# Layer 2's first product taken from layer 1's sums and rows, and stored blocks moved to the end of the pair loop

## The chip, the cores and the metric

The kernel runs on one core of one Trainium2 chip. The metric is the device time in microseconds of one execution, the median over several runs of the unchanged kernel: 566.83 us over 3 runs (566.69 to 569.11). Lower is better.

## The reference

The input is a matrix `x` of 3327 nodes by 64 features and a dense matrix `adj` (3327 x 3327, mostly zero). Four layers follow each other; each computes `x = layernorm(x + layer(x, adj))`. The change lies between the second and the third of them, which the reference numbers 1 and 2:

```python
# layer 1: hyperbolic attention
adj_att   = sigmoid(left + right.T) * adj
support_t = einsum('ij,ijd->id', adj_att, logmap(x_i, x_j))
x = layernorm(x + proj(expmap(x, support_t)))
# layer 2: two hops
for k in range(2):
    agg = adj @ x
    x = tanh(concatenate([agg, x], axis=1) @ W[k])
x = layernorm(x_in + x)
```

Since `concatenate([agg, x]) @ W[k]` is `adj @ (x @ W_top) + x @ W_bottom`, a hop of layer 2 needs the small product `x @ W_top` first, and then one pass over all of `adj`. "Layer 2's first product" is `x @ W_top` of hop 0.

## The kernel before, in words

The nodes are padded to 3328, which are 26 blocks of 128. A block of `adj` (transposed) is 128 rows of 3328 floats, 1.70 MB, one DMA from HBM. Four blocks (25 to 22, `kept`, `EARLY`) are loaded at the start and stay; all the others are fetched again in each layer. A row tile such as `x2`, `xc` or `lj` is [128, 26, 64]: one slot of 64 features for each block, blocks `b` and `b + 13` in neighbouring slots, so that a 128x128 transpose turns two blocks at once.

**Layer 1, the pair loop** (`near_sphere`, from L968). Two passes (`cp`) go over the 26 blocks; a pass takes half of the columns. One (pass, block) is a pair and has two tiles of 832 columns, 104 tiles in all. For each tile ACT makes the sigmoid (L1029, once a pair), POOL multiplies it by the block (`u`, L1040), PE makes distances (`pq`, L1053), DVE and ACT evaluate a cubic (`a` L1065, the square L1066, `v` L1074), and PE adds up `v` times the rows (`acc`, L1086). The order of blocks is written out in `order`; in both passes it begins with the four kept blocks. Streamed blocks go through four buffers (`at`, L1012) of a pool that stands beside the other work tiles. When the columns of a pass are summed, ACT copies them to `mT` (L1094), the sums, features by nodes. `ljT[0]` holds the nodes' rows in the same layout (differences to the last feature; the last feature's own row carries a norm term).

**Layer 1, the end** (`near_end`, L1286 to L1468). From `mT` PE makes the sums by node (`pm`, L1340) and their inner products with the rows (`pe`, L1350). ACT and DVE reduce them to about ten numbers per node. Then a chain of some 45 DVE instructions on [128, 26] tiles follows, with three ACT functions in it: a tanh (L1392) and two square roots (L1422). It ends in two factors per node, `al` and `be`: the layer's output is `x2 = al * M + be * xc` (L1463 to L1467), `M` the centred sums and `xc` the centred rows. Six matmuls of 512 columns whose result nobody reads (helper `awake`, L1326) stand in this chain. The same section centres layer 3's weights (`w3_dg`, L304).

**Layer 2** (`layers`, from L309). Hop 0 begins with `x2` turned by PE (`turned`, L345, copied by ACT, L349), the product with `W_top` (`top`, L355) copied to `lj` (L391), and the product with `W_bottom` added to the accumulators (`bottom`, L394). Then each block adds its 16 matmuls (`add`, L403). These beginnings are interleaved with the first two blocks. The blocks of hop 0 stand in `order`: four that were fetched ahead (`ready`, the `at_l` tiles), then a kept block and four streamed ones in turn (`bt_l` and `at_l`), 16 streamed in all, and two more kept ones at the end. Six blocks are asked for ahead of layer 2 by `blocks_ahead` (L1655): four `at_l` and two further `kept` ones (20, 21, pool `late`).

**What sets the order.** Each engine's instructions stand in the order written in the source within `manual_schedule`. DMAs of blocks all go through SP's queue, in order: one that waits for its buffer holds all behind it. Pools that are opened over the space of closed ones make the new tile's first writer wait for the last readers of the old one.

Of the kernel before, what the change touches and what calls it, by code (L numbers as in the profile page):

```python
# [15 lines left out]
ALU = mybir.AluOpType  # L16
# [57 lines left out]
def kernel(  # L74
# [234 lines left out]
    def layers(ctx, x2, x3, kept, ready, ahead_ctx, strm):  # L309
# [67 lines left out]
        with tc.tile_pool(name="l2p", bufs=2, space=PSUM, reuse_waits="tile") as l2p:  # L377
            for k in range(2):
# [49 lines left out]
                if k == 0:  # L428
# [20 lines left out]
                else:  # L449
# [13 lines left out]
                for i, jb in enumerate(order):  # L463
# [6 lines left out]
                    for c in range(CPH):  # L470
                        add(c, jb)
                    if k and jb in held and len(held) == 2:
                        for q in range(AHEAD + 3):
                            masks(q)
# [384 lines left out]
    with tc.tile_pool(name="l1", bufs=1) as l1:  # L859

        def l1_stat(name):
            return l1.tile([P, NB], F32, name=name)

        aa, g1, ga, xn, rxn, gs, gs2, gk, lpn = (
            l1_stat(name) for name in ("aa", "g1", "ga", "xn", "rxn", "gs", "gs2", "gk", "lpn")
# [107 lines left out]
        def near_sphere(mT, xm, sq_e, t_e):  # L973
# [3 lines left out]
            with tc.tile_pool(name="n1", bufs=1, reuse_waits="tile") as n1, tc.tile_pool(  # L977
# [3 lines left out]
            ) as n1c, ExitStack() as pairs:  # L981
                first_ps = ExitStack()
# [5 lines left out]
                ljT = [n1.tile([P, HALF], F32, name=f"ljT_{k}") for k in range(2)]  # L988
# [18 lines left out]
                def load(cp, jb):  # L1007
                    of = slice(cp * 2 * CW, (cp + 1) * 2 * CW)
                    if jb in kept:
                        return kept[jb].rearrange("p (h k) -> p h k", h=2)[:, :, of]  # L1010
                    at = n1w.tile([P, 2, 2 * CW], F32, tag="at", bufs=4, name=f"at1_{cp}_{jb}")
                    rows = adjT[jb * P : (jb + 1) * P, :].rearrange("p (h k) -> p h k", h=2)  # L1012
                    nc.sync.dma_start(at, rows[:, :, of])
                    return at

                tiles = [(cp, jb, ci) for cp in range(2) for jb in order for ci in range(2)]
# [53 lines left out]
                def gather(t, extra=()):  # L1070
# [10 lines left out]
                    if jb == order[0]:  # L1081
# [3 lines left out]
                    for h in range(2):  # L1085
                        nc.tensor.matmul(  # L1086
                            accs[cp, ci][h * D : (h + 1) * D, :], xv[:, slot(jb), :], w[:, h, :],
                            start=(jb == order[0]), stop=(jb == order[-1]),
# [3 lines left out]
                    if jb == order[-1]:  # L1092
# [102 lines left out]
                with tc.manual_schedule(  # L1195
# [47 lines left out]
                    for t in range(len(tiles)):  # L1243
# [13 lines left out]
                        if t == len(tiles) - 4:  # L1257
                            of = slice(0, 2 * CW)
                            nc.gpsimd.tensor_tensor(xm[:, of], mT[:, of], ljT[0][:, of], ALU.mult)
                        if t == len(tiles) - 3:  # L1260
# [15 lines left out]
                    of = slice(2 * CW, 3 * CW)  # L1276
                    nc.gpsimd.tensor_tensor(xm[:, of], mT[:, of], ljT[0][:, of], ALU.mult)
                    layer_3_constants()

                    nc.vector.tensor_scalar(gs, g1, MIN_NORM, -256.0, ALU.max, ALU.mult)  # L1280
                    vec(gk, gs, ga, ALU.mult)
                    vec(gs2, gs, gs, ALU.mult)
# [3 lines left out]
        def near_end(mT, xm, sq_e, t_e, x2):  # L1286
# [3 lines left out]
            with tc.tile_pool(name="l1e", bufs=1) as l1e, tc.tile_pool(  # L1290
                name="l1t", bufs=1, space=PSUM
            ) as l1t, tc.tile_pool(name="l1m", bufs=5, space=PSUM) as l1m:

                prod = l1e.tile([P, NB, D], F32, name="prod_xm")
                sqm = l1e.tile([P, NB, D], F32, name="prod_mm")
# [14 lines left out]
                def both(a, scalar, b, tag, op0, op1):  # L1310
# [5 lines left out]
                    engines={mybir.EngineType.PE, mybir.EngineType.Activation, mybir.EngineType.DVE}  # L1316
                )
                in_order.__enter__()
                gss = of(mul, gs, s, "gss")
                gks = both(gk, -2.0, s, "gks", mul, mul)  # L1320
                aav = lin(aa, 1.0 / D, LN_EPS, "aav")
                idle = l1t.tile([P, 512], F32, name="idle_e")

                def awake(t):

                    nc.tensor.matmul(  # L1326
                        idle[:NB, :], t, xc[:, :8].rearrange("p n d -> p (n d)"),
                        start=True, stop=True,
                    )

                gt = st("gt")
                p, q = st("p"), st("q")
                nc.vector.tensor_reduce(q[:, :12], sq_e, axis=AX.X, op=add)
                pms = {}

                def both_products(g, n):
# [9 lines left out]
                for g, n in threes[2:]:  # L1346
                    both_products(g, n)
                pe = l1t.tile([P, 9, 2], F32, name="pe")
                for k in range(9):
                    nc.tensor.matmul(  # L1350
                        pe[:, k], xm[:, k * P : (k + 1) * P], but_last, start=True, stop=True
                    )
                for g, n in threes[:2]:
                    both_products(g, n)
                for g, n in threes[2:]:
                    m = pms[g][:, :, :P].rearrange("p n (h d) -> p n h d", h=2)
                    nc.scalar.activation(by_half(sqm)[:, g : g + n], m, AF.Square)
                    if g > 6:
                        vec(by_half(prod)[:, g : g + n], m, by_half(xc)[:, g : g + n], mul)
                vec(gt[:, :12], t_e, gk[:, :12], mul)  # L1360
                for g, n in threes[2:]:
                    sl = slice(2 * g, 2 * (g + n))
# [4 lines left out]
                nc.vector.tensor_reduce(p[:, 18:], prod[:, 18:], axis=AX.X, op=add)  # L1367
                nc.vector.tensor_reduce(q[:, 12:], sqm[:, 12:], axis=AX.X, op=add)
                nc.vector.tensor_copy(p[:, :18], pe.rearrange("p n h -> p (n h)"))

                k = of(mul, p, gks, "k")
                vec(k, k, gt, add)
                gp = of(mul, p, gss, "gp")
                vec(p, p, s, mul)
# [7 lines left out]
                awake(u2)  # L1382
                centred_weights(l1t)
# [6 lines left out]
                awake(th)  # L1390
# [3 lines left out]
                nc.scalar.activation(warm_e[:, :1], ones, AF.Sqrt)  # L1394
                uy = of(mul, th, ux, "uy")
# [7 lines left out]
                al = of(mul, ca, gs, "al")  # L1403
                vec(be, be, ck, sub)
                alp = of(mul, al, p, "alp")
                bea = of(mul, be, aa, "bea")
                al2 = of(mul, al, al, "al2")
                n2 = both(alp, 2.0, bea, "n2", mul, add)
                vec(al2, al2, q, mul)
                vec(n2, n2, be, mul)  # L1410
                vec(alp, alp, bea, add)
                vec(n2, n2, al2, add)
                awake(n2)
                root = lin(n2, MIN_NORM * MIN_NORM, None, "root", ALU.max, ALU.bypass)
                dn = lin(y2, 1.0, None, "dn", add, ALU.bypass)
                stt(dn, uy, 2.0, dn, op0=mul, op1=add)
                sca(dn, dn, MIN_NORM, None, ALU.max)

                def rsqrt2(v, tag):

                    r0 = st(f"{tag}_r")
                    nc.scalar.activation(r0, v, AF.Sqrt)  # L1422
                    awake(v)
                    nc.vector.reciprocal(r0, r0)
                    t = of(mul, v, r0, f"{tag}_t")
                    vec(t, t, r0, mul)
                    stt(t, t, -3.0, r0, op0=add, op1=mul)
                    return t


                r0 = st("rdn")
                nc.vector.reciprocal(r0, dn)
                on = rsqrt2(root, "on")
# [296 lines left out]
```

## Time and profile before

| | us |
|---|---|
| median of 3 runs | 566.83 (566.69 to 569.11) |
| profiled execution, its own time | 566.58 |
| its span, first to last instruction | 564.9 |
| PE busy | 527.5 (93%) |
| DVE busy | 362.7 (64%) |
| ACT busy | 277.3 (49%) |
| POOL busy | 216.7 (38%) |
| HBM read | 143.23 MB, 255 GB/s over the span |

A page of the profile gives busy times by engine, the same in 40 slices of the span (14.1 us each), the chain of work that ended last, and groups of instructions by line. The timeline lists instructions with start and duration; `[2.66 <-DVE e_n]` behind a row is the idle time of that engine before it and who ended it. Several equal instructions in a row are merged (`x16`). `PEclk` is the clock that TensorE was granted, 1.00 being full. A name with a number stripped, such as `at_l` or `w_dg`, is the source's `at_l2` or `w2_dg`.

### The profile page before, as it was taken

The page shows a single profiled execution, that of the slowest core. Times are in us where ns is not written, and L with a number is a line of the kernel's source. Part 1 is how long each engine was busy: PE and PEld are TensorE (multiplying, and loading weights), DVE is VectorE, ACT ScalarE, POOL GpSimd, SP SyncE. Part 2 cuts the span into 40 slices and gives each one's busy share as a digit, 9 for nine tenths or more (in the row PEclk, how much of TensorE's full clock was granted, in tenths as well). Part 3 has the DMA queues.
Part 4 walks back from the last instruction along what each step waited for, and adds up shares of the span by engine and source line. Part 5 has one row for each costly group of instructions (what it writes and reads, how often), then busy time and mean ns, then how long its engine had stood idle before and what let it go on. Part 6 is the DMA issues. An engine that isn't in the chain of part 4 may idle for free.

```text
span 564.9 us, 7457 instructions
## 1 busy us (share of the span) xinstructions
PE 527.5 (93%) x2827; PEld 221.9 (39%) x2827; DVE 362.7 (64%) x527; ACT 277.3 (49%) x330; POOL 216.7 (38%) x134
## 2 busy tenths in 40 slices
PE   8899989999999999779999999999999999999992
PEld 5523222222222223444444454443455555545542
DVE  6899999999999999750000010400378888787834
ACT  4899999999999997350000000000274333343311
POOL 3799999999999999110000000000011000000000
PEclk9899999999999999999999999999999999999997
DMA  8986766660576671999999219999609986689801
GB/s 293 356 282 202 237 201 219 208 231 0 188 236 203 222 238 35 386 430 424 427 426 424 113 49 411 425 426 382 243 0 307 359 303 244 214 267 338 302 2 36
DMA packets 34037, 145.27 MB, mean 257 GB/s; under 512 B 10285, under 2 KB 11975, under 8 KB 28871
## 3 DMA queue, kind: packets, MB, share of 16 engines
q1 hardware_dynamic: 31655, 144.11, 69.5%
q10 hardware_dynamic: 2336, 0.59, 0.5%
q8 instruction: 24, 0.39, 0.3%
q14 instruction: 22, 0.18, 0.1%
HBM read 143.23 MB, written 0.87 MB: 255 GB/s over the span
## 4 chain that ended last, share of the span: by engine, by line
PE 63%; DVE 20%; ACT 8%; issue 5%; DMA 2%; DVEq 0%; POOL 0%; POOLq 0%
PE cnt L403 23%; PE pq L1053 12%; DVE v L1074 12%; PE cnt L498 11%; PE acc L694 6%; ACT sg L1029 4%; PE acc L709 3%; ACT pq L1066 2%; DVE a L1065 2%; DMA at_l<-in_adjT 2%; PE pn_l L355 1%; DVE w L511 1%; PE cnt L394 1%; DVE mask L337 1%; PE idle L889 1%
## 5 line engine op out<-in xcount | busy, mean ns | idle before, releaser
L1040 POOL TENSOR_TENSOR u<-sg,at 128x832 f32<-128x832 f32 x88 | 169.8, 1960 | 3.2 <-ACT sg L1029 2.7
L1053 PE MATMUL pq<-riT,ljT 64*128 64x416 f32 x416 | 100.2, 560 | 15.2 <-DVE v L1074 6.3
L1065 DVE SCALAR_TENSOR_TENSOR a<-pq,dl,u 128x832 f32<-128x832 f32 x104 | 111.8, 1076 | 3.0 <-PE pq L1053 2.9
L1066 ACT ACTIVATE pq<-pq,al,gas 128x832 f32<-128x832 f32 x104 | 104.9, 1010 | 15.2 <-DVE a L1065 14.2
L1074 DVE SCALAR_TENSOR_TENSOR v<-pq,a 128x832 f32<-128x832 f32 x104 | 105.5, 1014 | 1.1 <-ACT pq L1066 0.7
L1086 PE MATMUL acc<-v,xv 128*64 128x416 f32 x416 | 95.4, 538 | 0.1
L1029 ACT ACTIVATE sg<-lb,rb 128x1664 f32<-128x1664 f32 (+1 forms) x53 | 87.3, 1647 | 0.1
L403 PE MATMUL cnt<-at_l,lj 128*64 128x416 f32 x480 | 86.3, 513 | 0.6 <-DMA at_l<-in_adjT 0.6
L513 ACT ACTIVATE w<-cnt 128x832 int16<-128x832 f32 x55 | 47.2, 863 | 71.5 <-PE cnt L498 71.4
L478 ACT ACTIVATE hT<-cnt 128x416 f32<-128x416 f32 x8 | 4.1, 517 | 148.6 <-PE cnt L403 148.6
L625 POOL TENSOR_TENSOR s<-sq,s 128x384 bf16<-128x384 f32 (+1 forms) x4 | 4.1, 1026 | 188.0 <-ACT s L624 188.0
L511 DVE TENSOR_SCALAR w<-cnt 128x832 int16<-128x832 f32 x49 | 50.1, 1023 | 25.8 <-PE cnt L498 24.5
L1053 PEld LDWEIGHTS pq<-riT,ljT 64*128 64x128 f32 x416 | 31.5, 184 | 88.3 <-DVE v L1074 83.0
L391 DVE COPY lj<-pn_l 128x384 f32<-128x384 f32 (+2 forms) x8 | 4.3, 541 | 85.2 <-PE pn_l L355 85.2
L403 PEld LDWEIGHTS cnt<-at_l,lj 128*64 128x64 f32 x480 | 34.0, 137 | 50.0 <-issue 47.7
L498 PE MATMUL cnt<-mask,tri 128*128 128x416 bf16 x208 | 53.5, 339 | 0.1
L694 PE MATMUL acc<-w,s 128*128 128x416 bf16 x208 | 52.6, 339 | 0.5 <-DVE hid L766 0.5
L498 PE MATMUL cnt<-mask,rest 128*128 128x416 bf16 x200 | 51.6, 340 | 1.2 <-ACT w L513 0.6
L1086 PEld LDWEIGHTS acc<-v,xv 128*64 128x64 f32 x416 | 20.6, 134 | 61.0 <-issue 57.7
L337 DVE TENSOR_SCALAR mask<-ah 128x1664 bf16<-128x1664 f32 x42 | 43.4, 1033 | 0.0
L403 PE MATMUL cnt<-kept,lj 128*64 128x416 f32 x192 | 35.5, 513 | 0.0
L1040 POOL TENSOR_TENSOR u<-sg,kept 128x832 f32<-128x832 f32 x16 | 30.9, 1962 | 3.8 <-ACT sg L1029 3.8
(283 smaller groups left out, 390.2 us busy)
## 6 DMA issues: line engine op xcount, KB each, us to landing
at_l<-in_adjT SPq DMA_DIRECT2D x26, 1664.0 KB, 12.0
at<-in_adjT SPq DMA_DIRECT2D x44, 832.0 KB, 4.9
ah<-in_adjT SPq DMA_DIRECT2D x42, 832.0 KB, 6.4
bt_l<-in_adjT SPq DMA_DIRECT2D x8, 1664.0 KB, 10.0
kept<-in_adjT SPq DMA_DIRECT2D x6, 1664.0 KB, 8.8
lb<-lf_rows SPq DMA_DIRECT2D x2, 384.0 KB, 4.4
ljT<-ljT SPq DMA_DIRECT2D x4, 128.0 KB, 6.4
x<-in_x ACTq DMA_DIRECT2D x1, 416.0 KB, 5.4
```

The costliest lines, as they stand in the source:

```text
L337: nc.vector.tensor_scalar(mask[q], at, 0.0, None, ALU.not_equal)
L403: nc.tensor.matmul(acc[c][h * D : (h + 1) * D, :], hw[:, slot(jb), :], blocks[jb][:, o : o + CW], start=c not in begun, stop=last, skip_gr ...
L498: nc.tensor.matmul(cnt[c][:, e, :], mat, mask[q][:, of], start=start, stop=(mat is tri), skip_group_check=True,)
L511: nc.vector.tensor_scalar(w.bitcast(I16), cnt[c], 0.0, None, ALU.max)
L694: nc.tensor.matmul(acc[h, c][:, e, :], s12[:, slot(jb)].rearrange("p t d -> p (t d)"), ws[q, c][:, e, :], start=first, stop=last,)
L1029: nc.scalar.activation(sg[:, :, of], lbs[:, :, of], AF.Sigmoid, bias=rb[:, sl : sl + 1])
L1040: nc.gpsimd.tensor_tensor(u, sg[:, :, of], at[:, :, of], ALU.mult)
L1053: nc.tensor.matmul(pq[:, h, :], ljT[h != jb // NBH][rows, of], riT[rows, ch * CW : (ch + 1) * CW], start=True, stop=True,)
L1065: stt(a_s[t], pqs[t], dl[:, one], us.pop(t), op0=ALU.add, op1=ALU.mult)
L1066: nc.scalar.activation(pqs[t], pqs[t], AF.Square, bias=al[:, one], scale=gas[:, one])
L1074: stt(w, pqs.pop(t), CUBIC_REST, a_s.pop(t), op0=ALU.add, op1=ALU.mult)
L1086: nc.tensor.matmul(accs[cp, ci][h * D : (h + 1) * D, :], xv[:, slot(jb), :], w[:, h, :], start=(jb == order[0]), stop=(jb == order[-1]),)
```

## The change

1. Hop 0's `x2 @ W_top` is no longer made from the finished `x2`. PE multiplies the rows `ljT` by the centred `W_top` (`x_w`) and the sums `mT` by the centred and turned `W_top` (`m_w`) inside `near_end`, where the chain of small instructions runs; the two factors per node (now `alpha`, `beta`) are then put on both by DVE, straight into `lj`. `x2` itself is computed behind that, and its transposes and `bottom` come after the fourth, fifth and sixth block of hop 0.
2. `near_end` is put into one written order for POOL too: the products with `xm` are made by DVE, `pe` covers all 13 column blocks (26 matmuls for 18), the six matmuls of `awake` are gone, the chain between tanh and the second root is written otherwise, constants of the chain are made by POOL at the end of the pair loop, and ACT takes copies of `M` and of the products between its functions.
3. In the second pass the four kept blocks come last. The streamed `at` buffers move to a pool of their own (`n1r`, right side), and the two `late` blocks (20, 21) are asked for first and take that space.

The diff, cut to its core:

```diff
+                n1r = pairs.enter_context(
+                    tc.tile_pool(name="n1r", bufs=4, side="right", reuse_waits="tile")
+                )
-                    at = n1w.tile([P, 2, 2 * CW], F32, tag="at", bufs=4, name=f"at1_{cp}_{jb}")
+                    at = n1r.tile([P, 2, 2 * CW], F32, tag="at", name=f"at1_{cp}_{jb}")
-                tiles = [(cp, jb, ci) for cp in range(2) for jb in order for ci in range(2)]
+                orders = (order, sorted(order, key=lambda jb: jb in kept))
+                tiles = [(cp, jb, ci) for cp in range(2) for jb in orders[cp] for ci in range(2)]
...
+                            gp.tensor_scalar(gs, g1, MIN_NORM, -256.0, ALU.max, ALU.mult)
+                            gp.tensor_tensor(gk, gs, ga, ALU.mult)
...
+                            gp.tensor_tensor(rows_63, but_last[:, :1], but_last[:, 1:], ALU.add)
-                    of = slice(2 * CW, 3 * CW)
-                    nc.gpsimd.tensor_tensor(xm[:, of], mT[:, of], ljT[0][:, of], ALU.mult)
-                    layer_3_constants()
...
+                nc.vector.tensor_reduce(q[:, :12], sq_e, axis=AX.X, op=add)
+                x_times_m(2)
+                x_times_m(3)
+                m_and_t(6, 3)
+                m_and_t(9, 3)
+                m_and_t(12, 1)
+                p_of(0, NBH)
...
+                m_out(6, 3)
+                m_out(9, 3)
+                m_out(12, 1)
+                nc.scalar.activation(w3_dg, w3_dg, AF.Copy, scale=float(2**27))
...
+                first = in_bank("first_w")
+                nc.tensor.transpose(first[:, :P], all_m[:, :P], ident)
+                nc.tensor.matmul(
+                    first[:, P : 2 * P], center, w2_dg[:, 0, :], start=True, stop=True
+                )
+                m_and_t(0, 3)
...
+                nc.scalar.copy(all_mT, first[:, :P])
+                nc.scalar.activation(w_x, first[:, P : 2 * P], AF.Copy, scale=rows_63)
+                second = in_bank("second_w")
+                nc.tensor.matmul(second[:, :P], all_mT, w2_dg[:, 0, :], start=True, stop=True)
+                nc.tensor.matmul(second[:, P : 2 * P], center, w3_dg, start=True, stop=True)
+                xs = [in_bank(f"x_w_{g}") for g, _ in fours[:2]]
+                times(xs[0], ljT, w_x, *fours[0])
+                times(xs[1], ljT, w_x, *fours[1])
+                m_and_t(3, 3)
+                last_x = in_bank("x_w_12")
+                times(last_x, ljT, w_x, *fours[3])
...
-                awake(u2)
-                centred_weights(l1t)
...
                 nc.scalar.activation(th, arg, AF.Tanh, scale=-1.0)
                 warm_e = st("warm")
                 nc.scalar.activation(warm_e[:, :1], ones, AF.Sqrt)
+                nc.scalar.copy(w_m, second[:, :P])
+                m_out(0, 3)
...
+                r0, r = table_root(root, "on")
+                x_out(xs[0], *fours[0])
+                x_out(xs[1], *fours[1])
...
+                r0, t = table_root(var, "ln")
+                m_out(3, 3)
+                nc.scalar.copy(w3_dg, second[:, P : 2 * P])
+                x_out(last_x, *fours[3])
+                rest_x = in_bank("x_w_8")
+                mw = {b: in_bank(f"m_w_{b}") for b in (0, 3, 1, 2)}
+                times(mw[0], mT, w_m, *fours[0])
+                times(rest_x, ljT, w_x, *fours[2])
+                x_out(rest_x, *fours[2])
+                for b in (3, 1, 2):
+                    times(mw[b], mT, w_m, *fours[b])
...
+                for b, g, n in ((0, 0, 1), (0, 1, 3), (3, 12, 1), (1, 4, 4), (2, 8, 4)):
+                    sl = slots(g, n)
+                    pt = mw[b].rearrange("p (n d) -> p n d", d=D)
+                    pt = pt[:, sl.start - 8 * b : sl.stop - 8 * b]
+                    vec(pt, pt, one(alpha, sl), mul)
+                    vec(lj[:, sl], lj[:, sl], one(beta, sl), mul)
+                    vec(lj[:, sl], lj[:, sl], pt, add)
+                for g, n in threes:
+                    sl = slots(g, n)
+                    vec(x2[:, sl], x2[:, sl], one(alpha, sl), mul)
+                    vec(xc[:, sl], xc[:, sl], one(beta, sl), mul)
+                    vec(x2[:, sl], x2[:, sl], xc[:, sl], add)
...
+            for jb in range(NB - EARLY - LATE, NB - EARLY):
+                all_kept[jb] = block(late, jb, name=f"kept_{jb}")
             for jb in range(UNDER_WAY):
                 ready[jb] = block(strm, jb, tag="at", name=f"at_l2_0_{jb}")
...
-                if k == 0:
+                if k == 0 and not begun_here:
...
+                    if k == 0 and begun_here:
+                        if i == 3:
+                            turned(0)
+                            turned(1)
+                        if i == 4:
+                            turned(2)
+                            turned(3)
+                            turned(4)
+                        if i == 5:
+                            for c in range(CPH):
+                                bottom(c)
```

Here `times(pt, rows, w, g, n)` makes `n` products of 128x128, `x_out` and `m_out` are ACT copies out of PSUM, and `in_bank` takes one of four banks of the pool `l1w` in turn, so that a fifth tile waits until the first has been copied out. `m_and_t`, `p_of` and `t_of` are the former `both_products`, the `pe` loop and the `gt` products under new names.

## The prediction

> **What bounds the kernel now.** I read the page's slices first, then the table by stage, then the timeline from the end of the pair loop to the first blocks of layer 2.
>
> ```profile
> PE   8899989999999999779999999999999999999992
> 225.00:248.00 23.00, 16.51 (x93) 9.32 (x93) 18.30 (x87) 10.44 (x32) 3.90 (x7) 1.00 0.96 395
> 270.00:326.00 56.00, 56.00 (x324) 23.04 (x322) 0.00 (x0) 1.55 (x3) 0.00 (x0) 1.00 0.80 337
> 336.00:384.00 48.00, 48.00 (x276) 19.65 (x276) 6.08 (x7) 0.00 (x0) 0.00 (x0) 1.00 0.99 410
> ```
>
> The columns of a stage are its length, then busy time and count of PE, weight loads, DVE, ACT and POOL, the granted clock, the DMA share and GB/s. In layer 2 PE is never idle (56 of 56, 48 of 48). The dip is slices 17 and 18 (two 7s): between pair loop and layer 2 PE has 16.5 busy of 23, and much of that is matmuls nobody reads. There the chain of waits runs through small DVE instructions:
>
> ```profile
> 232.52 0.19 DVE L1302 TENSOR_TENSOR e_k<-e_p,e_gks 128x26 f32<-128x26 f32 x1
> 235.60 0.27 ACT L305 COPY both_m<-pw 128x128 f32<-128x128 f32 x1 [5.89 <-issue]
> 235.76 0.23 ACT L1392 ACTIVATE e_tanh<-e_th 128x26 f32<-128x26 f32 x1
> 238.31 0.23 ACT L1422 ACTIVATE e_on_r<-e_root 128x26 f32<-128x26 f32 x1 [0.81 <-DVE e_root L1307]
> 241.19 0.23 ACT L1422 ACTIVATE e_ln_r<-e_n 128x26 f32<-128x26 f32 x1 [2.66 <-DVE e_n L1441]
> 242.56 0.18 DVE L1445 SCALAR_TENSOR_TENSOR e_al<-e_ln_t,e_al 128x26 f32<-128x26 f32 x1
> 248.41 3.01 PE L403 MATMUL cnt<-at_l,lj 128*64 128x416 f32 x16
> 251.35 0.55 PE L345 MATMUL pt_x<-ident,x 128*128 128x128 f32 x3
> 256.66 2.96 PE L394 MATMUL cnt<-xc,w_dg 128*128 128x416 f32 x8
> ```
>
> Seen here: the factors per node are there at 242.7, and it takes 5.85 us more (multiply, turn, copy, product, copy) until the first block of layer 2 starts. Whatever starts that block earlier moves all that follows, because PE is full from there.
>
> **The change, part by part.**
>
> *Start of the chain.* `pe` grows to 26 matmuls. L1350's 18 took 2.07 us, so 0.107 each and 0.25 for the last; from 229.07 that ends at 232.0. DVE has finished its reductions by 231.1 (it drops the 832-element `prod` and 0.67 of a reduction, takes 2 x 0.59 for two products of 416), so the chain begins at 232.1 for 232.52. In before the tanh argument was ready at 234.78 but the tanh ran at 235.76: ACT held the copy L305, which waited for a PE product behind an `awake`. Now ACT has 1.2 us of `M` copies (0.48, 0.48, 0.27, released by `pe` from 231.2 on), then 0.2 to 0.27 each for `w3_dg`, `all_mT`, `w_x`, and is free at 233.5. The argument, 2.2 us after the chain's start, is the later one: tanh at 234.35, **1.4 us earlier**.
>
> *Tanh to first root.* 22 small instructions for 18, at the 0.11 to 0.22 that the rows show: 3.0 us for 2.55, **0.45 later**. Behind the tanh ACT loads a table (1.28), then copies `w_m` and one `M` part (0.75): free at 236.8, root wanted at 237.35.
>
> *First to second root.* One reciprocal (0.32) and 6 dependent steps instead of two reciprocals and 12: 1.7 us for 2.88, **1.2 earlier**. In it ACT does two copies of 512 (0.58 each, as L1164 shows), ending at 238.75; the second root is wanted at 239.05. That cover is 0.3 us thin; without it the rest would be the root's delay. To `alpha` 1.27 instead of 1.37: it starts at **240.3**, for 242.56.
>
> *Factors to first block.* The first 128 columns of `lj` need three DVE instructions (0.29 is the row of a 128x128 multiply out of PSUM, and 0.2 between starts): ready at 241.25. But PE comes later. Its last 17 products (`m_w` 13, `x_w` 4) stand ahead of the first block in its queue and begin when the first bank is copied out, at 238.2. L1340's 7 products took 1.86, 0.25 each: 4.25, and some 0.3 for two waits on ACT copies: **PE is free at 242.8**. This, and not the chain, starts the first block: 248.41 - 242.8 = **5.6 us earlier**. The bounds: if the products overlap their waits fully, DVE's 241.25 (7.2 us); if each product costs what L355's 3 did with their fill and drain (0.94, 0.31 each), 243.8 (4.6 us). I take 242.8, since the products run in groups of four, nearer to the seven of L1340.
>
> *Inside hop 0.* Removed: 13 `top` products and their waits, 2.04 us at 251.35 and 0.33 at 256.33. Added there: 13 transposes at 0.17 (L345, 3 in 0.52), 2.2 us. `bottom` (2.9) stays. DVE's five triples of `lj` and five of `x2` end near 253, before the fourth block ends (254). I count **0.3 earlier**; if the transposes wait for each other's ACT copies (two banks, 0.48 a copy), 0.5 later.
>
> *Stored blocks last.* A pair costs the same either way (POOL's multiply is 1960 ns with `at`, 1962 with `kept`). The last streamed pair now ends four pairs (15.4 us) earlier, so blocks 20 and 21 are asked for at about 207.8 instead of 223.26 and 229.36, while DMA was idle. No time by itself; it pays for the earlier start:
>
> ```profile
> 222.00:224.00 2.00, 1.90 (x12) 0.40 (x8) 2.00 (x3) 1.02 (x1) 2.00 (x2) 1.00 0.00 0
> 227.55 1.77 SPq L209 DMA_DIRECT2D at_l<-in_adjT  x4
> 312.00:316.00 4.00, 4.00 (x26) 1.70 (x24) 0.00 (x0) 0.00 (x0) 0.00 (x0) 1.00 0.60 253
> ```
>
> The four `at_l` still wait for the last tile's products, so they are asked for at 227.55 as now; SP holds nothing else. Data flow from 228.8. A block of 1.70 MB at 425 GB/s takes 4.0 us (4.1 for the first four): `at_l` 0 is there at 233, the sixteenth streamed block of hop 0, the twentieth in this queue, at 228.8 + 16.4 + 64 = 309.2. PE wants it after 23 blocks of 2.8 (384 matmuls took 67.2 us, 16 each), transposes and `bottom`: 242.8 + 64.4 + 5.1 = 312.3. Before, the last ended near 314.4 and was wanted at 318.4. So 3.1 us of margin are left of 4; with the two early blocks still in this queue (8 us) there would be none. In hop 1 the buffers come free by PE's own progress; it moves as a whole.
>
> At this place the Trainium skill speaks against the change. Measured here are 424 to 432 GB/s in the stages from 240 on. "DMA: Bandwidth & Descriptors", section "Where 436 GB/s comes from", gives about 358 GB/s as the limit of HBM reads per core; at that rate, by estimate, 20 blocks would take some 95 us, the last would land at 324, and hop 0 would end later than before. The measured rate decides.
>
> *POOL.* Eight small instructions (0.22 to 0.28 each by L1209 to L1211) behind the `xm` product that ends at 225.15: done at 227.3, first read at 229.4. The two casts for layer 3 stand ahead of the pair loop in the built order, 0.6 us in 3.6 + 2.1 us of POOL idleness. Nothing.
>
> *TensorE's clock.* The six `awake` matmuls (1.04 us each) go, and `pe` moves only 2 columns a matmul.
>
> ```profile
> 12.00:14.00 2.00, 1.77 (x14) 1.35 (x14) 1.70 (x9) 1.48 (x2) 0.00 (x0) 0.98 1.01 433
> 14.00:16.00 2.00, 2.00 (x10) 2.00 (x11) 1.41 (x13) 0.71 (x2) 0.73 (x3) 0.50 1.13 296
> ```
>
> After 24 matmuls of 4 columns (10.8 to 13) the granted clock fell to 0.50, and it stayed there from 13.9 to 17.2. `pe` is such a stretch, of 2.9 us, so a stretch at half clock from about 232 is likelier than not; it slows `x_w`, which have 1.2 us of slack at 237, by up to 1.7 us. I charge **0.4**. "TensorE: Matmul & The Clock Gate", Part 1, tells the same story by windows of about 3.4 us that run free; by that rule the products (full from 232 to 237 and from 238.2 on) would bring the clock back after one window, and the loss on `x_w` would be at most 1.7.
>
> **Sum.** 5.6 + 0.3 - 0.4 = 5.5 us off the profiled execution's 566.58 (span 564.9 and 1.7 around it): **561.1 us**. The median of the runs shown is 566.83, 0.25 above; I leave the forecast at 561.1.
>
> **Rivals.**
> 1. *The transfers end last in hop 0.* For: only 3.1 us of margin, and 223 to 240 ran at 343 GB/s. Against: that stretch had one block in flight at first, and now four queue at once. At 400 GB/s a block costs 4.26, the last lands at 314.0, 1.7 past PE's wish: 562.8.
> 2. *Half clock over the last 17 products.* For: the queue of PE is empty from about 237 to 238.2 and the `awake`s are gone. Against: 5 us of products before. Price 1.7 to 2.5: 563.2.
> 3. *Half clock from 232 into layer 2*, the slower side. If products of 128 columns count too little, 19 products from 232.1 at 0.5 us end at 241.6, the last 17 at 250.3, and the first block loses 1.7 more: 252 against 248.4, 3.5 slower: 570. It decides when the clock is not back to 1.00 by about 238. Against: between 234 and 242 PE was busy 5.1 us of 8 in before and kept 1.00.
> 4. *The early blocks do nothing*, since their request sits behind a later wait: the order of SP's queue puts only `at` blocks before them, so this costs nothing by the order; were it so, the last block would land 8 us later, 4.9 past PE's wish: 566.0, no change. Counted with rival 1.
>
> **How the numbers follow.** Forecast (560 to 562.4) 0.70; rival 1, 0.11; rival 2, 0.11; rival 3, 0.08. The range reaches from DVE's bound (7.2 us off, 559.4) to rival 2 with its dearer price (564.2). Faster by over 0.5% (about what a measurement of this kernel can tell from no change) is below 564.0: the forecast, nearly all of rival 1 and half of rival 2, 0.86; within 0.5%: 0.06; slower: 0.08.
>
> **What would show it.** `e_tanh` near 234.4, the roots near 237.4 and 239.1, `alpha` near 240.3; the first `cnt` matmul of layer 2 near 242.8, right behind the last `m_w`; `kept` asked for at 208; no DMA wait of PE in hop 0; hop 0 of 78 us. Wrong would be: ACT's copies ending behind a root's argument, a clock of 0.5 beyond 236, or `cnt` waiting for `at_l` or `bt_l`.

## The result, and the profile after

The changed kernel takes **561.99 us** (median of 4 runs, 561.51 to 562.48) beside 567.28 for the kernel before on the same chip (566.69 to 569.11): ratio 0.990, 95% interval 0.988 to 0.993. The forecast was 561.1, the range 559.4 to 564.2. In a second set of runs (4) the same kernel gave 561.47 (560.66 to 562.12), ratio 0.988 (0.985 to 0.991). The profiled execution took 562.28 with a span of 560.5, so the span lost 4.4 us, not the 5.5 of the prediction.

First the page of the kernel after, then three stages (length, busy time of PE, weight loads, DVE, ACT, POOL, clock, DMA share, GB/s):

```profile
PE   8989989999999999999999999998989999999992
PEclk9899999999999999899999999999999999999997
225.00:248.00 23.00, 23.00 (x164) 17.94 (x164) 19.50 (x83) 10.20 (x27) 2.13 (x9) 0.93 0.85 346
270.00:326.00 56.00, 55.84 (x320) 23.81 (x318) 1.38 (x2) 2.07 (x4) 0.00 (x0) 1.00 0.72 302
336.00:384.00 48.00, 48.00 (x278) 19.65 (x276) 5.79 (x6) 0.00 (x0) 0.00 (x0) 1.00 1.01 424
```

The two 7s in PE's row are gone: PE is busy for all 23 us of the seam, the stretch between the pair loop and layer 2. Two 8s are new behind it, in slices 28 and 30; the first of these is the end of hop 1. The seam in the timeline:

```profile
232.19 0.19 DVE L1440 TENSOR_TENSOR e_k<-pe,gks 128x26 f32<-128x26 f32 x1 [1.19 <-PE pe L1391]
234.31 0.23 ACT L1479 ACTIVATE e_tanh<-e_th 128x26 f32<-128x26 f32 x1 [1.12 <-DVE e_th L1477]
237.12 0.23 ACT L1512 ACTIVATE e_on_s<-e_root 128x26 f32<-128x26 f32 x1 [0.54 <-DVE e_root L1338]
237.25 1.05 ACT L1417 COPY lj<-x_w 128x512 f32<-128x512 f32 x2
237.87 1.16 PE L1411 MATMUL m_w<-w_m,mT 128*128 128x128 f32 x8
238.74 0.23 ACT L1512 ACTIVATE e_ln_s<-e_var 128x26 f32<-128x26 f32 x1 [0.44 <-DVE e_var L1525]
239.75 2.17 PE L1411 MATMUL m_w<-w_m,mT 128*128 128x128 f32 x18
240.01 0.19 DVE L1543 SCALAR_TENSOR_TENSOR dl<-e_n_r,e_al 128x26 f32<-128x26 f32 x1
240.83 0.29 DVE L1552 TENSOR_TENSOR lj<-lj,m_w 128x128 f32<-128x128 f32 x1
241.86 11.39 PE L403 MATMUL cnt<-at_l,lj 128*64 128x416 f32 x64
```

DVE's first rows are ready at 240.83 + 0.29 = 241.1, and the first block starts at **241.86**, behind the last `m_w` (before: 248.41). What follows, in the order of time: the requests of the two stored blocks and of the first four streamed ones, and the only two waits of PE for a transfer in layer 2; below them the one such wait of the kernel before.

```profile
207.86 0.84 SPq L209 DMA_DIRECT2D kept<-in_adjT  x2
227.62 2.15 SPq L209 DMA_DIRECT2D at_l<-in_adjT  x4
312.10 3.01 PE L403 MATMUL cnt<-at_l,lj 128*64 128x416 f32 x16 [0.16 <-DMA at_l<-in_adjT]
391.15 3.01 PE L403 MATMUL cnt<-at_l,lj 128*64 128x416 f32 x16 [2.15 <-DMA at_l<-in_adjT]
```

```profile
395.72 3.01 PE L403 MATMUL cnt<-at_l,lj 128*64 128x416 f32 x16 [0.59 <-DMA at_l<-in_adjT]
```

So the account of the span is: the first block starts 6.55 earlier; hop 0 (first block to hop 1's first product, L355) takes 78.77 for 78.33, 0.44 lost, so that hop 1 starts at 320.6 for 326.7; the wait in hop 1 is 2.15 for 0.59, **1.56 lost**; layer 3 and the rest take 169.3 for 169.1, 0.17 lost. 6.55 - 0.44 - 1.56 - 0.17 = 4.4.

### The profile page after: what moved, and what is told of

The parts are those of the page before. It is cut to its first block, busy times and chain, and to the rows that moved or that the text cites. A ratio compares the mean times of both kernels' runs of the same rounds, so it can differ in the third digit from the quotient of the medians.

```text
span 560.5 us, 7513 instructions
## 1 busy us (share of the span) xinstructions
PE 527.3 (94%) x2854; PEld 226.6 (40%) x2854; DVE 368.2 (66%) x532; ACT 278.1 (50%) x328; POOL 215.7 (38%) x138
## 4 chain that ended last, share of the span: by engine, by line
PE 61%; DVE 20%; ACT 8%; DMA 6%; issue 3%; DVEq 0%
PE cnt L403 20%; PE pq L1075 12%; DVE v L1096 12%; PE cnt L513 11%; PE acc L709 6%; DMA at_l<-in_adjT 5%; ACT sg L1051 4%; PE acc L724 3%; ACT pq L1088 3%; DVE a L1087 2%; DVE w L526 1%; PE cnt L394 1%; DVE mask L337 1%; DMA x<-in_x 1%; PE pm L1367 1%
## 5 line engine op out<-in xcount | busy, mean ns | idle before, releaser
L391 DVE COPY lj<-pn_l 128x512 f32<-128x512 f32 (+1 forms) x4 | 2.4, 592 | 73.9 <-PE pn_l L355 73.9
L1108 PEld LDWEIGHTS acc<-v,xv 128*64 128x64 f32 x416 | 20.6, 134 | 61.0 <-issue 57.8
```

The source lines that it names most:

```text
L1108: nc.tensor.matmul(accs[cp, ci][h * D : (h + 1) * D, :], xv[:, slot(jb), :], w[:, h, :], start=(jb == orders[cp][0]), stop=(jb == orders[c ...
```

## The experiments

Theory after the profile: (a) the product from layer 1's sums brings the first block forward, and PE's own work sets it there; (b) the early blocks pay only because the first block comes early; (c) the loss in hop 1 is the tail of the stream, which the loading of instructions delays. Rivals: the product alone is the gain; the half clock costs part of it; the loss in hop 1 is another block's or belongs to the execution. "Chain start" is `e_k`.

**1. Stored blocks not last** (early blocks undone, all else as after).

```diff
-orders = (order, sorted(order, key=lambda jb: jb in kept))
+orders = (order, order)
```

> The changed kernel with one thing undone: the second pass begins with the four kept blocks again, as in the first. Theory (the early request of blocks 20 and 21 pays for the earlier start): both are asked for at about 223.3 instead of 207.9, so 22 blocks of some 4.05 us stand in one stream from 224.5; the last streamed block of hop 0 lands at 314 plus the lag of the slowest DMA engine (about 3 us), and PE wants it at 312: a wait of 3 to 5 us in hop 0, 565 to 567 us. Rival (transfers are hidden anyway): no wait, 562.0.

565.15 us (564.16 to 566.15), ratio to before 0.9945 (0.992 to 0.997). The first block is as early as after (242.34), `kept` is asked for at 223.80, and PE waits in hop 0 four times where the kernel after waits 0.16. The rows of PE:

```profile
252.13 3.01 PE L403 MATMUL cnt<-at_l,lj 128*64 128x416 f32 x16 [0.98 <-DMA at_l<-in_adjT]
300.12 3.02 PE L403 MATMUL cnt<-at_l,lj 128*64 128x416 f32 x16 [0.24 <-DMA at_l<-in_adjT]
312.11 3.01 PE L403 MATMUL cnt<-at_l,lj 128*64 128x416 f32 x16 [0.60 <-DMA at_l<-in_adjT]
316.09 3.01 PE L403 MATMUL cnt<-at_l,lj 128*64 128x416 f32 x16 [0.96 <-DMA at_l<-in_adjT]
```

The sum of these waits is 2.8 us; hop 0 as a whole takes 82.3 us for 78.8, and the difference of the medians is 3.2. The two early blocks are worth that, where the first block comes early.

**2. First product from `x2`** (`x_w`, `m_w` and what serves them removed, `x2` made first, turned and multiplied as in the kernel before; the early blocks stay).

```diff
-times(xs[0], ljT, w_x, *fours[0])
...
-x_out(xs[0], *fours[0])
...
-for b in (3, 1, 2):
-    times(mw[b], mT, w_m, *fours[b])
...
-layers(x2, xc, True, *blocks)
+layers(x2, xc, False, *blocks)
```

> The changed kernel without part 1: no x_w and m_w products, x2 is finished first, and hop 0 begins with its transposes, top and bottom as before the change. The new chain and the early blocks stay. Theory (the chain gave 2.5 us, the product out of sums and rows the rest): the factors are there at 240.0 to 240.3 and 4.5 to 5 us later the first block starts, at 244.5 to 245.3, for 248.4 before and 241.9 in the changed kernel; 564 to 565 us. Rival (the chain alone is the gain, the products only fill PE): 562. Rival (the product alone is the gain): 567.

567.35 us (566.88 to 569.64), ratio 0.9998 (0.998 to 1.0016): missed by 2.4 us. The time is that of the last rival, no gain at all. The trace does have a gain: the first block starts at 247.10 for 248.41 in the kernel before, and the last product of the whole program ends at 553.6 for 554.95, both 1.3 us earlier. The 1.3 us are lost behind that product: from there to the end of the span this profile has 11.5 us, the kernel before 9.9, all other profiles 9.6 to 10.2. Seven loads of instructions of 8 KB stand there for six in every other profile, the last at 564.5. Whether this load is what makes the end longer was not tested, so this run's time says little about the seam.

It does not show either what the early blocks are worth without the product, as no run takes them out of it. The kernel before bears on that: it asked for them late, and PE waited for no transfer in its hop 0.

Part of the late first block is the clock. In this run PE has nothing to do from 236.3 to 242.1 and is granted 0.50 from 240 to 246; from the first turn of `x2` to the first block it takes 4.96 us, 4.0 in the kernel before.

```profile
242.14 0.88 PE L345 MATMUL pt_x<-ident,x 128*128 128x128 f32 x3 [5.80 <-DVE x L1523]
244.00:246.00 2.00, 2.00 (x12) 2.00 (x11) 1.96 (x4) 0.68 (x2) 0.00 (x0) 0.50 1.02 433
247.10 3.01 PE L403 MATMUL cnt<-at_l,lj 128*64 128x416 f32 x16
```

**3. The same, kept awake** (the products that nobody reads put back, also behind `n2` and in both roots, with `xc` as their moving operand).

```diff
 vec(u2, u2, gq, add)
+awake(u2)
...
 vec(th, th, xn, mul)
+awake(th)
...
 stt(alpha, n_r, -0.5, al, op0=mul, op1=mul)
+awake(alpha)
```

> The run e2_product_from_x2 (layer 2's first product made from x2, as before the change, all else as after) with the five products back that gave TensorE something to do during the chain in the kernel before. e2 gave 567.35 us with the first block at 247.1; its clock was 0.5 from 240 to 247, in which the transposes and products of x2 took 4.96 us, against 4.0 us in the kernel before at clock 1.00. Theory: the half clock took 1.0 us from e2, so the clock is 1.00 here, the first block begins at 246.0 to 246.3, and the time is 566.2 to 566.6. Making the first product from layer 1's sums is then worth about 4.3 us of block time by itself. Rival: the clock cost nothing, since VectorE's rows of x2 (242.0 to 246.6) set those products: first block 247.0, time 567.2 to 567.5.

566.31 us (565.64 to 570.04), ratio 0.998 (0.996 to 1.0005). The time is as expected, the place is not: the first block begins at 247.35. The clock is 1.00 from 238 on, and turn to first block takes 4.18 us (0.8 less than in run 2). But the last added product reads `xc`, which DVE then overwrites, and DVE waits for it; counted from the chain's start, the first turn comes 0.8 later (10.65 us for 9.81):

```profile
241.88 0.56 DVE L1535 TENSOR_TENSOR xc<-xc,xf 128x384 f32<-128x384 f32 x1 [0.76 <-PE idle_e L1452]
```

So the clock was worth 0.8 us to run 2, and the cure cost as much. From chain start to first block the way by `x2` takes 14.8 us in both runs, and by this sum 14.0 without the half clock, against 9.67 after: the product from the sums is worth 4.3 to 5.1 us of first block. The kernel before takes 15.9; the remaining 1.1 to 1.9 us go to the rest of the change, the new order of the chain above all.

**4. `pe` moving 130 columns** (128 of them zeros, so the same values).

```diff
-but_last = const.tile([P, 2], F32, name="but_last")
+but_last = const.tile([P, P + 2], F32, name="but_last")
...
-pe[:, k], xm[:, k * P : (k + 1) * P], but_last,
+pe[:, 2 * k : 2 * k + P + 2], xm[:, k * P : (k + 1) * P], but_last,
```

> The kernel after, with the 26 products pe moving 130 columns (two wanted, 128 zeros) instead of 2. Theory: the half clock of one 3.41 us window (0.57 in 232 to 236) comes from TensorE's stretch of 2-column products at 227 to 231, and it costs the last products 0.9 to 1.7 us. Then the clock stays 1.00 in 232 to 236, and the work that TensorE does from 232 on ends 0.9 us or more sooner; but the wider products take 0.13 us for 0.11 each, which puts the chain's start (232.2) later by up to 0.4 us, so the first block of layer 2 begins at 241.3 to 241.8 (now 241.86), and the time is 561.5 to 562. Rival A: the clock is lowered by something else: it stays at 0.57 in that place, first block at 242.2. Rival B: the clock is full and the first block is no sooner, since VectorE's last rows (241.1) set it: 241.4 to 241.5.

One run, 560.9 us. First two windows of the kernel after, then the first of them in this run, and its `m_w`:

```profile
232.00:234.00 2.00, 2.00 (x12) 2.00 (x13) 1.77 (x15) 1.18 (x5) 0.00 (x0) 0.57 1.00 421
236.00:238.00 2.00, 2.00 (x19) 1.86 (x18) 1.64 (x14) 1.46 (x6) 0.00 (x0) 1.00 1.00 426
```

```profile
232.00:234.00 2.00, 2.00 (x19) 1.93 (x18) 1.27 (x11) 1.57 (x6) 0.00 (x0) 1.00 0.98 414
238.40 1.16 PE L1411 MATMUL m_w<-w_m,mT 128*128 128x128 f32 x8 [1.51 <-ACT lj L1417]
242.40 11.39 PE L403 MATMUL cnt<-at_l,lj 128*64 128x416 f32 x64
```

The half clock is gone, so in this order of the program the 2-column products brought it (run 5 has the same products without it); and `x_w` takes 1.95 us for 16 instead of 2.54. Yet the first block starts 9.67 us after the chain's start, exactly as in the kernel after (241.86 - 232.19 = 9.67; here 242.40 - 232.73). PE, faster, waits 1.5 us for ACT's copy of the first `x_w` bank. The theory that PE alone sets the first block falls: PE was busy without a gap in the kernel after because its backlog at half clock ended in the very moment (237.9) when the bank came free. Rival B had the effect, a first block no sooner, with the wrong cause: VectorE's rows are ready at 241.37 + 0.29 = 241.7 there, 0.7 ahead of it.

**5. `first_w` in PE's gap ahead of it.**

```diff
+first = in_bank("first_w")
+nc.tensor.transpose(first[:, :P], all_m[:, :P], ident)
...
 m_and_t(6, 3)
 m_and_t(9, 3)
...
-first = in_bank("first_w")
-nc.tensor.transpose(first[:, :P], all_m[:, :P], ident)
...
```

> The kernel after, with the transpose and the product first_w, and their two copies by ACT, put ahead of m_and_t(6, 3), into TensorE's gap at 226.6 to 227.4. Theory: TensorE is busy without a gap from 228 to 242 and alone sets the first block; work of 0.5 to 0.8 us that goes into an idle place ahead of that brings the first block 0.4 to 0.5 us forward, to 241.4 (where VectorE's rows, ready at 241.1, and the eviction set it), and the time to 561.5 to 561.8. Rival: VectorE's chain sets the first block, and it stays at 241.8 to 241.9.

One run, 562.45 us; missed. The chain starts 1.0 us later (25.3 us after the request of `kept`, 24.3 in the kernel after), PE runs dry at 236.4 and waits 1.88 us for the same copy, and the clock falls to 0.50 behind it. Behind the 26 products of 2 columns, which run here from 229.59 to 232.55, it stayed at 1.00:

```profile
232.00:234.00 2.00, 2.00 (x19) 2.00 (x20) 1.30 (x12) 1.03 (x4) 0.00 (x0) 1.00 1.05 434
238.33 1.87 PE L1411 MATMUL m_w<-w_m,mT 128*128 128x128 f32 x8 [1.88 <-ACT lj L1417]
240.00:242.00 2.00, 2.00 (x11) 2.00 (x11) 1.82 (x9) 0.18 (x2) 0.00 (x0) 0.50 1.02 433
```

The 17 products behind the wait take 5.6 us instead of 4.0, and the first block begins 11.3 us after the chain's start. The prediction's rival 2, half clock over the last 17 products, did not come in the kernel after, but this is it, and its price is 1.6 us.

**6. The copy ahead of the root** (run 4, and ACT empties the first bank before the first root).

```diff
+x_out(xs[0], *fours[0])
 r0, r = table_root(root, "on")
-x_out(xs[0], *fours[0])
```

> e3 (wide first columns, so the clock is 1.00 throughout) with one more edit: ACT copies the first bank of x_w out before the first root instead of after it. In e3 TensorE waited 1.51 us for that copy, and the first block of layer 2 began at 242.40, 9.67 us after the chain's start (e_k at 232.73); in the kernel after it was 241.86, also 9.67 after its own (232.19), at half clock and without a wait. Theory: what sets the first block is the copy that frees the bank, behind the root on ACT, plus 3.5 to 4.0 us of products behind it, not TensorE's backlog and not the clock. ACT is idle for 0.54 us ahead of the root and the copy takes 0.53, so the products begin 0.7 us sooner, the root is late by 0.1 at most, and the first block begins 9.1 to 9.3 us after the chain's start (VectorE's first rows then set it). Rival: the second bank's copy or VectorE's rows held it all along: 9.6 to 9.7.

One run, 561.07 us. The products begin earlier, but the first block comes 9.57 us after the chain's start, a gain of 0.1 where 0.4 to 0.6 was expected:

```profile
236.72 0.60 ACT L1417 COPY lj<-x_w 128x512 f32<-128x512 f32 x1
237.38 1.16 PE L1411 MATMUL m_w<-w_m,mT 128*128 128x128 f32 x8 [0.77 <-ACT lj L1417]
239.81 2.27 PE L1411 MATMUL m_w<-w_m,mT 128*128 128x128 f32 x18 [0.39 <-ACT both_m L1529]
242.02 1.27 PE L403 MATMUL cnt<-at_l,lj 128*64 128x416 f32 x6
```

The wait moved: now the last nine products (`x18`, two instructions each) wait for the bank of `second_w`, which ACT copies out behind the *second* root. Two copies of banks behind two roots on ACT were nearly equally late. And the 0.1 is no gain over the kernel after: its chain starts 0.1 later, behind the wider products, and from the request of `kept` to the first block both take 34.0 us.

**7. Two stored blocks instead of three at hop 1's end.**

```diff
-n_end = 3 if k else 2
+n_end = 2
```

> The changed kernel, but hop 1 keeps two stored blocks for its end instead of three, so that the last streamed block is wanted 2.8 us later. Theory (hop 1 ends on that block's landing): the wait of 2.15 us goes, 560.0 us. Rival (the three blocks at the end cover the start of layer 3, whose squares and roots then show): 562 or more, with PE idle between 393 and 420.

565.06 us (564.39 to 566.60), ratio 0.996 (0.994 to 0.998), 3.1 slower than after. The edit does not do what was expected of it: the third stored block goes behind the last streamed one in the written order, so PE wants that block no later, at 389.0 as in the kernel after. The wait of 1.26 instead of 2.15 comes from a stream that is shorter by 1 us, not from a later wish. The loss is in layer 3: it starts with less work of layer 2 under it, and PE waits for the chain of its norms (0.63 in the kernel after), with a half clock behind it:

```profile
390.23 3.01 PE L403 MATMUL cnt<-at_l,lj 128*64 128x416 f32 x16 [1.26 <-DMA at_l<-in_adjT]
409.80 3.09 PE L580 MATMUL both<-both_m,hT 128*128 128x256 f32 x8 [2.69 <-DVE xc L613]
412.00:414.00 2.00, 2.00 (x8) 0.91 (x7) 0.45 (x1) 0.60 (x1) 0.00 (x0) 0.53 0.00 0
```

**8 and 9. Another phase of the instruction loads** (80, then 110 tiny products at TensorE's start, for two of the three there).

```diff
+tiny = const.tile([P, 1], BF16, name="tiny")
+nc.vector.memset(tiny, 1.0)
...
-for _ in range(3):
-    nc.tensor.matmul(idle, ident, center_4, start=True, stop=True)
+for _ in range(80):
+    nc.tensor.matmul(idle[:1, :1], tiny, tiny, start=True, stop=True)
+nc.tensor.matmul(idle, ident, center_4, start=True, stop=True)
```

> The changed kernel with 80 one-column bf16 matmuls (160 PE instructions) at the very start in place of two of the three filler matmuls there. Theory (the last transfer of hop 1 lands late because 16 KB instruction fetches, about 1 us each and one per 22 us, stand in the stream of one DMA engine; three of them fell into hop 1's stream, two before the change): the fetches come some 14 us earlier relative to hop 1, so that two fall into it, and PE's wait for the last streamed block is 0.6 to 1.1 us instead of 2.15. Rival (the wait is the stream's mean rate or contention): 2.0 to 2.3 us as now. The start may itself be up to 2 us longer, which says nothing on this.

> The kernel after with 110 tiny products in place of two of the three at TensorE's start, which moves the loads of TensorE's instructions, one for 256 of them, some 19 us earlier against its work (and puts the whole body 6.6 us later). In hop 1 they then come at 319, 344, 367 and 389 us as seen from the work of the kernel after, in place of 341, 363 and 385.6. Theory: a load that falls within 5 us ahead of a block with thin margin costs the wait; then no wait before the last block, and 0.6 to 0.8 us at the last. Rival: the lag is not due to that load: 1.2 to 2.2 us at the last block, as in the kernel after, e1, e3 and e6.

One run each, 566.27 and 566.44 us, with the chain's start 4.8 us later. In run 8 PE waits 1.44 and 0.59 us in hop 1, in run 9 three times 0.6 (371.87, 383.86, 395.85). The last wait came out at 0.6 as expected both times, but waits that the kernel after does not have stand ahead of it, and the sums (2.0 and 1.8) are hardly below 2.15. The theory is not borne out.

**10. The kernel after again.**

> The kernel after, unchanged: a second profile of it, for the wait at the end of hop 1. If the lag of one DMA engine there (last packets 2.5 us behind the bulk) belongs to the order of the kernel's own requests and instruction loads, it comes again: 2.0 to 2.2 us of wait, and 562.0 us. If it changes from execution to execution, the wait is anything from 0.6 to 2.2 us.

561.47 us; the wait is 2.13 us (2.15 in the first profile). So in two profiles it belongs to the program, not to the execution.

**11. The last streamed block worked into hop 1's end.**

```diff
+tail = order.pop() if k else None
...
 def chunk_end(c):
+    late_c = k and c == CPH - 1
     for jb in end:
-        add(c, jb, jb == end[-1])
+        add(c, jb, jb == end[-1] and not late_c)
+    if late_c:
+        add(c, tail, True)
     nc.scalar.activation(nxt[:, c * CW : (c + 1) * CW], acc[c], AF.Tanh)
+    if late_c:
+        for other in range(CPH - 1):
+            add(other, tail)
...
 if k:
+    blocks[tail] = block(strm, tail, tag="at", name=f"at_l2_{k}_{tail}")
```

> The kernel after, with the last streamed block of hop 1 worked into the end: chunk 3's three stored blocks are taken ahead of it, then its four products, the rest as before. Theory: in hop 1 TensorE is ready for this block at 389.0 and waits 2.15 us, as one DMA engine lags and the last packets land at 390.7. The stored products of chunk 3 (12 of 0.19 us, 2.3 us) cover that: the wait is under 0.2 us, chunk 3 is complete some 4 us sooner, all of layer 3 begins 2 us sooner, and the time is 559.8 to 560.4. Rival A: layer 3's start is set by its own chain on ScalarE and VectorE and by its loads, and the 2 us is lost there as idle time of TensorE in 398 to 420: 561.5 to 562. Rival B: the landing moves later with it, and the wait comes back in another place: 562.

The wait is gone, since chunk 3's stored blocks run in it:

```profile
388.54 2.27 PE L403 MATMUL cnt<-kept,lj 128*64 128x416 f32 x12
390.63 3.10 PE L403 MATMUL cnt<-at_l,lj 128*64 128x416 f32 x16
```

In the profiled execution (559.81 us) chain start to end takes 326.2 us, 328.3 and 328.0 in the two profiles of the kernel after. The median of 6 runs is 560.82 (559.81 to 562.52), 0.4 above the expected 559.8 to 560.4, ratio to before 0.989 (0.986 to 0.991): lower than the kernel after's, but the intervals overlap.

**12. Runs 4, 6 and 11 together.**

> e13 with the edit of e11 (last streamed block of hop 1 taken after chunk 3's stored blocks). If both gains stand side by side, 0.4 us at the first block and 1.2 to 2.2 us at the end of hop 1: no DMA wait of TensorE at the end of hop 1, span 2 us below that of the kernel after for the same start of the work, 559.5 to 560.5 us. Rival: hop 1's stream, not TensorE, sets the end of layer 2, and what is won at the first block is lost again there: as e11, 560.8.

The profiled execution took 559.35 (325.5 from chain start to end, 2.4 to 2.7 less than after), the median of 4 runs is 561.09 (559.35 to 561.44), the kernel after beside it on the same chip 561.47. The median missed the expected 559.5 to 560.5. In the trace both edits stand side by side; that the kernel is faster than the one after is not shown.

## Why the prediction was right, and where it was not

**The chain.** Start 232.19 (said 232.1), tanh 234.31 (234.35), roots 237.12 and 238.74 (237.35 and 239.05), `alpha` 240.01 (240.3). Every step came within 0.3 us.

**Factors to first block: right in kind, mis-sized.** PE's last products stand ahead of the block and begin when ACT frees the first bank: said, and runs 4 and 6 show it. But they begin at 237.87, when the first of the two copies is done, not at 238.2; the 17 took 3.99 us (0.235 each), not 4.25 plus 0.3 for waits. 241.86 for 242.8: 0.95 more gained, that is 6.55 where 5.6 stood in the sum. (The 5.85 us of before count from 242.56, where the last factor starts; from its end at 242.74 it is 5.7.)

**Clock: the half clock came, and cost the first block nothing.** The clock fell to 0.57 in 232 to 236, as said from the row of the 4-column products, and `x_w` lost 0.6 us. The charge of 0.4 was wrong: run 4 without the half clock has the same 9.67 us. The Trainium skill ("TensorE: Matmul & The Clock Gate", Part 1) has windows of about 3.4 us; the low stretch in the trace is 3.41 us long, and the clock was back after one of them.

**Inside hop 0.** Said 0.3 earlier (its own terms, 2.04 + 0.33 - 2.2, give 0.17), measured 0.44 later. What stands between the blocks (turns, `bottom`) is even: 5.2 us for 5.3, with 0.24 of it a wait for a bank at 258.05. 0.16 is the DMA wait at 312.10; the rest lies in the blocks' own starts, 0.1 here and there.

**Stored blocks last.** Asked for at 207.86 (said 207.8), worth 3.2 us (run 1). The margin of 3.1 us was wrong: all but 16 packets of the sixteenth streamed block had landed by 309.7 (309.2 was worked out), the last of those 16 at 311.6, 5.6 us behind the block ahead of it and not 4.0. PE wanted it at 311.9. The rate was right (the 20 blocks took 83.0 us from first to last packet, where an estimate of 95 spoke against the change); what the sum lacks is the late last packets. The same error stands in the reading of the kernel before, where the mean DMA share of 0.60 over 312 to 316 was taken for an end of the stream at 314.4: its last packet landed at 317.0. The margin there was 1.3 us, not 4.

**"In hop 1 ... it moves as a whole": the step that failed.** The start of the stream did move with PE: its first packet comes at 330.7 for 336.8, and PE is ready for the last streamed block at 389.0 for 395.1, both 6.1 us earlier. But the stream became longer, 60.0 us for 58.5. Up to its thirteenth block the two are alike (53.6 us); the blocks come 4.0 us apart (380.3, 384.3). The last one comes at 390.7, 6.35 us behind the one ahead of it, 4.83 in the kernel before. There was no margin to take this: the kernel before already waited 0.59 us for this block, a row of its trace that the prediction did not use. At the end of the stream one DMA engine works alone:

```profile
389.00:390.00 1.00, 0.00 (x0) 0.00 (x0) 0.00 (x0) 0.00 (x0) 0.00 (x0) 1.00 0.06 27
```

0.06 is one of 16 engines: four packets of 0.50 us, one behind the other. From first to last packet hop 1's stream takes 58.5 us (before, run 2), 58.7 to 59.3 (runs 3 to 7) or 59.9 to 60.1 (after, after again, runs 1, 8 and 9). PE's waits in hop 1 follow it: in all twelve profiles that have such a wait, their sum is that length less 57.8 to 58.3 us. Rival 1, the transfers ending last, thus came true in hop 1, where the prediction did not look, at 1.56 us.

**Sum.** Expected 5.6 + 0.3 - 0.4 = 5.5; measured 6.55 - 0.44 - 1.56 - 0.17 = 4.4. The terms that were too small a gain (0.95 at the first block) or too large a charge (0.4 for the clock) cover the losses in hop 0 and hop 1 in part, so that the forecast came within 0.9 us of the median partly by luck. The medians moved by 5.3, as the profiled execution of before was below its median and that of after above.

**Rivals.** 2 and 3 did not come (clock 1.00 from 236 on). 4 is excluded by run 1. The upper end of the range does not follow from rival 2: its dearer price gives 561.1 + 2.5 = 563.6, not 564.2.

**What stays open.** Why the last engine ends so late in hop 1's stream: by the times of the packets 1.6 to 1.8 us behind the next one in the kernel after, in its second profile and in run 1, 0.6 to 0.8 in runs 4, 6 and 7, while in the kernel before three end within 0.1 us. TensorE's instructions are loaded in pieces of 16 KB, in layer 2 one about every 22 us, in which PE starts some 255 matmuls and weight loads. A load takes 0.9 to 1.1 us in this stream. Three fall into it in the kernel after, two in before and in run 2. But runs 4, 6 and 7 have the same three at the same places within 0.6 us and streams 1 us shorter, and runs 8 and 9 have two and streams as long as the kernel after's. The late end was not traced to a cause, only covered (run 11). Also open is why the end of run 2 took 1.6 us longer than that of the kernel before.

## What to carry to other kernels

An engine that is busy without a gap need not be the bound: take its load away and see whether the end moves (run 4: 0.00 of 0.6 us). When a gain brings a stage forward, check the margin of every stream that feeds what follows, at its last block and for all engines' ends, not for the mean rate: hop 1 gave back 1.56 of 6.55 us. A prefetch is worth what the earlier consumer makes it worth: 3.2 us with the early product, while the kernel before had no wait in hop 0 that it could have taken away. And when an edit's time says "no gain", see where in the trace the gain is lost: in run 2 it was 1.3 us up to the last product and gone behind it.

## What the hardware showed beyond that

A gap of 1.9 us in PE's work (run 5) or 2.7 us (run 7) was followed by half clock over the work right behind it, and added 1.6 us in run 5; the 1.5 us of run 4 were not. Products with 2 moving columns, PE "busy" all along, were followed by the same in the kernel after and in every other run that has the 26 of them, run 5 excepted, and run 4 took it away by moving 130. Each of these low stretches is 3.41 us long by the trace's clock records, that of run 2 from 239.65 on is 6.83. And 130 columns instead of 2 cost hardly anything: 26 took 3.07 us for 2.96.
